# GpSimd's order fixed to the source's, the statistics placed behind a scan, and the next chunk's preparation shifted by half a state

## The chip, the core and the metric

The kernel runs on one core of a Trainium2 chip. The core has five engines that each work through a queue of their own, in order: PE (TensorE, matrix products; its weight loads are shown as PEld), DVE (VectorE), ACT (ScalarE), POOL (GpSimd) and SP (SyncE, which only issues transfers here). An instruction waits at the head of its queue until the semaphores it needs are set, and everything behind it waits with it. The metric is the time on the device in microseconds (us).

## What is computed

A net of four layers on an input of 4 images, 128 channels, 64 x 64 pixels. The change lies in the part of the program that computes the first two layers together. Layer 0 is a state space model (256 inner channels, 16 states) over the 4096 pixels of an image, and layer 1 a hypergraph convolution; cut to what matters here:

```python
# layer 0, per image
xc    = silu(conv(xs) + conv_b)
x_dbl = xc @ x_proj_w.T                      # 8 + 16 + 16 rows: dt, B, C
delta = softplus(dt_r @ dt_proj_w.T + dt_proj_b)
hn = exp(delta * A) * hprev + (delta * xc) * B_t     # for each of 16 states, along the pixels
y  = sum over states of hn * C_t
x  = ((y + xc * D) * silu(zg)) @ out_proj_w.T + x
# layer 1, per image, on the normalized x
incidence = (dist < THRESHOLD)               # 4096 x 4096
edge = incidence^T @ xe / deg_e
vert = incidence @ edge / deg_v
out  = vert + xf
y = batchnorm(out)                           # mean and variance over all images
x = x + y * sigmoid(y)
```

Layers 2 and 3 (attention and experts) follow and are not touched.

## The kernel before

`layers01` (from L79) is one program of Python generators. `layer0()` (L378) yields after each half state: an image is cut into 8 chunks of 512 columns, a chunk has 16 states, and a state has two halves `h` of 128 channels each. `layer1(b, ...)` (L469) yields the weight of the work that it has just emitted. The driver at L697 to L723 first emits image 0 of layer 0 alone; then, for images 1 to 3 of layer 0, it emits one half state, raises `self.tick` by one, runs the deferred pieces that are due, and emits as much of layer 1 of the image before as belongs to that half state; at last layer 1 of image 3 alone. In this text chunks of layer 0 are counted through from 0 to 31, so image 1 starts with chunk 8.

For a state `n` of a chunk:

- `rows` (L280) loads B and C of the state, repeated over the partitions, into `bt` on SP's queue, three states ahead; there are five buffers.
- `drive` (L289) makes `db` = `dx` x B on GpSimd, one state ahead; `db` has two buffers, so that of state j+2 needs both scans of state j done.
- `state` (L293) makes two exponentials into the PSUM tile `hs` on ScalarE (L303; two buffers), a scan for each half on VectorE (L309), and after the second one a copy of the last column (`carry`, L318) and the product `ho` = `hs` x C (L319). For images 1 to 3 GpSimd then adds `ho` to the running sum of its eight states (L324, L326); states 0 and 8 only start a sum. For image 0 six of the sixteen products are GpSimd's (L314, L315).
- `steps` (L390) hangs the rest of layer 0 on half states `u` = 0 to 31 of a chunk. The list `slots` gives the half states in which the eleven steps that prepare the next chunk are emitted: load, project, conv, small (the small projection's matrix products, L242), rows_out (its copy L246 on ScalarE, and the store that `rows` of the next chunk reads), delta, two activations, exp, ln, and inputs (L271 and L273 on GpSimd: `dl` and `dx` for the next chunk).

Layer 1 of an image has a part in which token blocks are prepared, compared (L541 on PE, L544 on VectorE) or turned from earlier results (L553, L557), with the edge sums of the panel before (L564, L571 to L582) between them; and a vertex part (L654 on) that works through 8 column chunks. GpSimd's share in it is: the remainder of the tokens in half precision (L506), the scaling of the edges `ed` (L580), their remainder (L582), and the addition of the input to the vertex result `rb` (L681). ScalarE's L581 waits for L580. VectorE's product L680, GpSimd's L681 and VectorE's statistics L684 follow each other; L680 and L681 are emitted one tick after a column chunk's matrix products, L684 six ticks after them.

What sets the order in each queue: a planner of the framework orders the instructions of each engine by when it believes them ready, with the source's order as the priority. ScalarE is an exception: each of its instructions in this part is passed through `act` (L187), which makes it depend on the one before, for the order alone and with no semaphore. PE, VectorE, GpSimd and SP are left to the planner. So the source's place of an instruction is not its place in the queue.

Of the kernel before, what the change touches and what calls it, by code (L numbers as in the profile page):

```python
# [12 lines left out]
ALU = mybir.AluOpType  # L13
# [4 lines left out]
P = 128  # L18
# [13 lines left out]
def bc(ap, n):  # L32

    return ap.unsqueeze(1).to_broadcast([ap.shape[0], n, ap.shape[1]])
# [7 lines left out]
class Net:  # L42
# [36 lines left out]
    def layers01(self):  # L79
# [11 lines left out]
        with ExitStack() as ctx:  # L91
# [90 lines left out]
            late = ctx.enter_context(tc.tile_pool(name="late", bufs=1))  # L182


            order = []

            def act(i):  # L187


                if order:  # L190
                    tc.add_manual_dep(
                        i.ins, order[-1].name,
                        mybir.DependencyInfo(mybir.DependencyClass.NoSync, mybir.DependencyReason.DATA),
                        reason="order",
                    )
                order[:] = [i.ins]


            waiting = []
# [11 lines left out]
            def before(b, c):  # L211

                s = dict(b=b, c=c)
                t0 = c * T

                def load():
                    xt = s["xt"] = w2.tile([P, T + 3], F32, tag="xt", name="xt")
                    if c == 0:
                        nc.vector.memset(xt[:, 0:3], 0.0)
                        nc.sync.dma_start(xt[:, 3:], a["x"][b, :, 0:T])  # L220
                    else:
                        nc.sync.dma_start(xt, a["x"][b, :, t0 - 3 : t0 + T])

                def project():
                    xt = s["xt"]
                    s["ps"] = [ps.tile([P, T], F32, tag="ps", name="ps_c") for h in range(2)]
                    for h in range(2):
                        for j in range(4):
                            nc.tensor.matmul(  # L229
                                s["ps"][h], wc[:, h, j, :], xt[:, j : j + T], start=j == 0, stop=j == 3  # L230
                            )

                def conv():
                    xc = s["xc"] = w2.tile([P, 2, T], F32, tag="xc", name="xc")
                    for h in range(2):
                        act(nc.scalar.activation(xc[:, h, :], s["ps"][h], AF.Silu, bias=vec[:, h, 4:5]))

                def small():
                    xc = s["xc"]
                    px = s["px"] = ps.tile([P, T], F32, tag="ps", name="ps_xd")  # L240
                    for h in range(2):
                        nc.tensor.matmul(px[:40, :], xpT[:, h, :], xc[:, h, :], start=h == 0, stop=h == 1)  # L242

                def rows_out():
                    xd = s["xd"] = w2.tile([40, T], F32, tag="xd", name="xd", bufs=1)
                    act(nc.scalar.copy(xd, s["px"][:40, :]))  # L246
                    bcd = s["bcd"] = dp.tile([2 * DS, T], F32, tag="bcd", name="bcd")
                    nc.scalar.dma_start(bcd, xd[DR:40, :])

                def delta():  # L250
                    s["ps"] = [ps.tile([P, T], F32, tag="ps", name="ps_d") for h in range(2)]
                    for h in range(2):
                        nc.tensor.matmul(s["ps"][h], dtT[:, h, :], s["xd"][0:DR, :], start=True, stop=True)


                def parts(h):
                    if h == 0:
                        s["dl"] = w2.tile([P, 2, T], F32, tag="dl", name="dl")
                        s["sp"] = late.tile([P, 2, T], F32, tag="sp", name="sp")
                    act(nc.scalar.activation(s["sp"][:, h, :], s["ps"][h], AF.Abs, bias=vec[:, h, 5:6]))  # L260
                    act(nc.scalar.activation(s["dl"][:, h, :], s["ps"][h], AF.Relu, bias=vec[:, h, 5:6]))

                def exp():
                    act(nc.scalar.activation(s["sp"], s["sp"], AF.Exp, scale=-1.0))

                def ln():
                    act(nc.scalar.activation(s["sp"], s["sp"], AF.Ln, bias=1.0))

                def inputs():
                    dl = s["dl"]  # L270
                    nc.gpsimd.tensor_tensor(dl, dl, s["sp"], ALU.add)  # L271
                    dx = s["dx"] = w2.tile([P, 2, T], F32, tag="dx", name="dx")
                    nc.gpsimd.tensor_tensor(dx, dl, s["xc"], ALU.mult)  # L273

                return s, [
                    load, project, conv, small, rows_out, delta, lambda: parts(0), lambda: parts(1), exp, ln,
                    inputs,
                ]

# [8 lines left out]

            def drive(s, n):  # L289
                db = s["db", n] = w2.tile([P, 2, T], F32, tag="db", name="db")  # L290
                nc.gpsimd.tensor_tensor(db, s["dx"], bc(s["bt", n][:, 0, :], 2), ALU.mult)  # L291

            def state(s, n, h):  # L293

                b, c, db = s["b"], s["c"], s["db", n]
                if h == 0:
                    hs = s["hs"] = aps.tile([P, 2, T], F32, tag="hs", name="hs")  # L300
                    s["ho", n] = w2.tile([P, 2, T], F32, tag="ho", name="ho", bufs=6)
                    for k in range(2):
                        act(nc.scalar.activation(hs[:, k, :], s["dl"][:, k, :], AF.Exp, scale=A[:, k, n : n + 1]))  # L303
                hs, ho = s["hs"], s["ho", n]
                ct = bc(s["bt", n][:, 1, :], 2)
                split = b == 0 and n in TO_POOL
                init = 0.0 if c == 0 else carry[:, n, h : h + 1]
                to = ho if split else hs
                nc.vector.tensor_tensor_scan(to[:, h, :], hs[:, h, :], db[:, h, :], init, ALU.mult, ALU.add)  # L309
                if h == 0:  # L310
                    return
                if split:
                    if c < NT - 1:
                        nc.gpsimd.tensor_copy(carry[:, n, :], ho[:, :, T - 1])  # L314
                    nc.gpsimd.tensor_tensor(ho, ho, ct, ALU.mult)  # L315
                    return
                if c < NT - 1:
                    nc.vector.tensor_copy(carry[:, n, :], hs[:, :, T - 1])  # L318
                nc.vector.tensor_tensor(ho, hs, ct, ALU.mult)  # L319
                if b == 0 or n % G == 0:  # L320
                    return
                if n % G == 1:
                    s["sum", n // G] = w2.tile([P, 2, T], F32, tag="ho", name="ho_s", bufs=6)
                    nc.gpsimd.tensor_tensor(s["sum", n // G], ho, s["ho", n - 1], ALU.add)  # L324
                else:
                    nc.gpsimd.tensor_tensor(s["sum", n // G], s["sum", n // G], ho, ALU.add)  # L326

            def skip(s):

# [48 lines left out]
            def layer0():  # L378
# [6 lines left out]
                count = len(todo) * DS  # L385
                at = lambda i: (todo[i // DS][0], i % DS)

                slots = dict(zip((9, 14, 16, 18, 19, 20, 22, 23, 24, 25, 26), range(11)))

                def steps(k, u):  # L390

# [77 lines left out]
            def layer1(b, rstd, nmr):  # L469
# [18 lines left out]
                def tokens(c, sq):  # L488
# [14 lines left out]
                    hi = xs[:, 4 * c : 4 * c + 4, 0:P]  # L503
                    lo = xs[:, 4 * c : 4 * c + 4, P + 1 : 2 * P + 1]
                    later(2, lambda: act(nc.scalar.copy(hi, xe)))
                    later(3, lambda: nc.gpsimd.tensor_tensor(lo, xe, hi, ALU.subtract))  # L506

                def row(c, sq=None):

# [49 lines left out]
                def edges(inc, ed, c, i):  # L559
# [9 lines left out]
                    def parts():  # L569
                        both = pe[:, : 2 * P + 2].rearrange("p (k c) -> p c k", k=2)  # L570
                        nc.vector.reduce_sum(ed[:, i, :], both, axis=AX.X)  # L571
                        if i == 3:

                            rd = rdeg[:, 4 * c : 4 * c + 4]
                            nc.vector.tensor_scalar(rd, ed[:, :, P], 1.0, None, ALU.max)
                            nc.vector.reciprocal(rd, rd)  # L576
                            e = ed[:, :, :P]
                            hi = es[:, 4 * c : 4 * c + 4, 0, :]
                            lo = es[:, 4 * c : 4 * c + 4, 1, :]
                            nc.gpsimd.tensor_tensor(e, e, bc_last(rd, P), ALU.mult)  # L580
                            later(3, lambda: act(nc.scalar.copy(hi, e)))  # L581
                            later(4, lambda: nc.gpsimd.tensor_tensor(lo, e, hi, ALU.subtract))  # L582

                    later(2, parts)

# [68 lines left out]
                for c in range(NCH):  # L654
# [23 lines left out]

                    def mean(c=c, rb=rb, pv=pv):
                        nc.vector.scalar_tensor_tensor(rb, pv, top, rb, ALU.mult, ALU.mult)  # L680
                        nc.gpsimd.tensor_tensor(rb, rb, xn[c], ALU.add)  # L681

                    def finish(c=c, rb=rb):
                        nc.vector.bn_stats(stats[:, b, c, :], rb)  # L684
                        nc.sync.dma_start(self.hg[b][:, c * CH : (c + 1) * CH], rb)

                    due()
# [874 lines left out]
```

## Time and profile before

| | us |
|---|---|
| median of three runs | 4104.38 (4102.41 to 4105.93) |
| profiled execution, its own time | 4105.69 |
| its span | 4103.9 |
| layer 0 of image 0 alone | 45 to 562 |
| layer 0 of images 1 to 3 beside layer 1 of images 0 to 2 | 562 to 2824 |
| layer 1 of image 3 alone | 2824 to 3312 |
| layers 2 and 3 | 3312 to 4104 |
| busy in all: PE, DVE, ACT, POOL | 3456.7, 3001.7, 2034.9, 2460.4 |

The times of the stages are from the span's start. In the middle stage each of PE, VectorE and GpSimd is busy for about 82% of the time, but not at the same places: the stage repeats itself once for each image, 754 us long, and every image has a stretch of its own for comparing, for the edges and for the vertices. A row of waits reads: the engine and the instruction that waited, the engine and the instruction that ended the wait, the sum in us, how often, the longest. In the timeline the idle time before an instruction stands in brackets, with what ended it.

### The profile page before, as it was taken

What the parts mean: (1) busy time and instruction counts of PE and PEld (TensorE: products, weight loads), DVE (VectorE), ACT (ScalarE), POOL (GpSimd) and SP (SyncE); (2) the same over time, 40 slices, a digit from 0 to 9 for tenths busy, and PEclk for the clock granted to TensorE, in tenths of its full rate; (3) what the DMA queues carried; (4) which work ended last, traced back from release to release, by engine and by line L of the source; (5) the groups of instructions that cost most, each with busy time, mean ns of one, the idle gap of its engine ahead of it and who ended that gap; (6) DMA issues with size and microseconds to landing.
All of it is one profiled execution on the core that took longest, in us unless ns stands there. A gap on an engine that the chain in (4) does not pass through costs nothing. (4 is left out here: it accounts for less than half of the span.)

```text
span 4103.9 us, 48550 instructions
## 1 busy us (share of the span) xinstructions
PE 3456.7 (84%) x17255; PEld 1931.4 (47%) x17255; DVE 3001.7 (73%) x4628; ACT 2034.9 (50%) x3364; POOL 2460.4 (60%) x1242
## 2 busy tenths in 40 slices
PE   6878767888889788888977888887999979998989
PEld 2323323344543334455433444543567448765864
DVE  5888889999666899975679998664642067665764
ACT  4556554445644555555444455642223158842951
POOL 5998989888678898986879888674100020001300
PEclk8898888899999899999988999999999989999999
DMA  3545544455436454543644455447121420046138
GB/s 101 149 148 155 151 122 126 130 143 152 118 123 199 116 139 130 147 138 87 213 135 130 131 146 145 115 134 246 52 73 55 127 100 11 12 140 218 27 109 298
DMA packets 263845, 532.71 MB, mean 130 GB/s; under 512 B 22794, under 2 KB 25266, under 8 KB 262578
## 3 DMA queue, kind: packets, MB, share of 16 engines
q1 hardware_dynamic: 255666, 519.09, 42.3%
q10 hardware_dynamic: 7936, 10.52, 0.7%
q8 instruction: 136, 2.23, 0.2%
q14 instruction: 107, 0.88, 0.1%
HBM read 451.80 MB, written 77.73 MB: 129 GB/s over the span
## 5 line engine op out<-in xcount | busy, mean ns | idle before, releaser
L291 POOL TENSOR_TENSOR db<-dx,bt 128x1024 f32<-128x1024 f32 x512 | 1202.9, 2352 | 349.5 <-DVE hs L309 204.4
L309 DVE TENSOR_TENSOR_SCAN hs<-hs,carry,db 128x512 f32<-128x512 f32 x812 | 1033.9, 1282 | 257.1 <-ACT hs L303 176.0
L303 ACT ACTIVATE hs<-dl,A 128x512 f32<-128x512 f32 x1024 | 706.0, 692 | 773.1 <-DVE ho L319 721.2
L541 PE MATMUL ps_g<-xn 128*128 128x512 f32 x1152 | 603.5, 654 | 121.3 <-DVE inc L544 95.3
L326 POOL TENSOR_TENSOR ho_s<-ho_s,ho 128x1024 f32<-128x1024 f32 x288 | 677.5, 2352 | 11.7 <-DVE ho L319 6.5
L319 DVE TENSOR_TENSOR ho<-hs,bt 128x1024 f32<-128x1024 f32 x464 | 563.3, 1214 | 1.6
L564 PE MATMUL ps_ed<-xs,inc 128*128 128x258 f16 x4096 | 508.8, 284 | 41.8 <-DVE inc L544 20.2
L564 PEld LDWEIGHTS <-inc 128*128 128x128 fp8e4 x4096 | 414.7, 102 | 160.5 <-issue 88.8
L544 DVE SCALAR_TENSOR_TENSOR inc<-ps_g,hcl,hb 128x512 fp8e4<-128x512 f32 x576 | 418.6, 735 | 26.3 <-PE ps_g L541 12.6
L541 PEld LDWEIGHTS ps_g<-xn 128*128 128x128 f32 x1152 | 214.4, 203 | 439.3 <-DVE inc L544 213.1
L557 ACT CAST inc<-ps_t 128x512 fp8e4<-128x512 f32 x448 | 231.7, 601 | 299.3 <-PE ps_t L553 277.5
L347 PE MATMUL ps_y<-ho,cst 128*128 128x512 f32 x512 | 274.6, 680 | 108.9 <-POOL ho L315 91.5
L672 PE MATMUL ps_v<-inc_v,es 128*128 128x512 fp8e4 x1536 | 344.9, 383 | 18.0 <-DVE rb L680 18.0
L672 PEld LDWEIGHTS <-es 128*128 128x128 f16 x2048 | 203.2, 100 | 287.8 <-issue 65.2
L229 PE MATMUL ps_c<-xt,wc 128*128 128x512 f32 x512 | 234.2, 611 | 4.1 <-DVE inc L544 2.1
L347 PEld LDWEIGHTS ps_y<-ho,cst 128*128 128x128 f32 x512 | 105.5, 215 | 269.0 <-POOL ho L315 121.9
L1231 POOL CAST b1h<-b 128x512 bf16<-128x512 f32 x2 | 1.3, 648 | 302.1 <-DMA b<-in_L_ffn_weight 302.1
L580 POOL TENSOR_TENSOR ed<-ed,rdeg 128x512 f32<-128x512 f32 x32 | 33.2, 1038 | 247.6 <-DVE rdeg L576 247.6
L309 DVE TENSOR_TENSOR_SCAN hs<-hs,db 128x512 f32<-128x512 f32 x116 | 141.3, 1223 | 43.4 <-POOL db L291 36.9
L571 DVE TENSOR_REDUCE ed<-ps_ed 128x129 f32<-128x258 f32 x128 | 52.9, 413 | 159.5 <-PE ps_ed L564 159.5
L229 PEld LDWEIGHTS ps_c<-xt,wc 128*128 128x128 f32 x512 | 99.3, 197 | 127.7 <-issue 114.9
L1467 POOL MEMSET ob<- 128x256 f32 x4 | 1.2, 311 | 262.1 <-PE ps_t L1410 262.1
(317 smaller groups left out, 5463.7 us busy)
## 6 DMA issues: line engine op xcount, KB each, us to landing
bt<-bcd SPq DMA_DIRECT2D x512, 512.0 KB, 4.9
w<-in_L_ffn_weight SPq DMA_DIRECT2D x64, 1024.0 KB, 11.1
inc<-inc SPq DMA_DIRECT2D x192, 256.0 KB, 2.4
inc_v<-inc SPq DMA_DIRECT2D x96, 512.0 KB, 6.4
strip<-inc SPq DMA_DIRECT2D x84, 256.0 KB, 3.0
x<-x ACTq DMA_DIRECT2D x32, 256.0 KB, 5.7
xn<-x SPq DMA_DIRECT2D x32, 256.0 KB, 5.5
hg<-rb SPq DMA_DIRECT2D x32, 256.0 KB, 2.7
```

The source lines that it names most:

```text
L229: nc.tensor.matmul(s["ps"][h], wc[:, h, j, :], xt[:, j : j + T], start=j == 0, stop=j == 3)
L291: nc.gpsimd.tensor_tensor(db, s["dx"], bc(s["bt", n][:, 0, :], 2), ALU.mult)
L303: act(nc.scalar.activation(hs[:, k, :], s["dl"][:, k, :], AF.Exp, scale=A[:, k, n : n + 1]))
L309: nc.vector.tensor_tensor_scan(to[:, h, :], hs[:, h, :], db[:, h, :], init, ALU.mult, ALU.add)
L319: nc.vector.tensor_tensor(ho, hs, ct, ALU.mult)
L326: nc.gpsimd.tensor_tensor(s["sum", n // G], s["sum", n // G], ho, ALU.add)
L347: nc.tensor.matmul(s["y"][h], self.ident, t[:, h, :], start=False, stop=n == DS - 1 and k == len(terms) - 1,)
L541: nc.tensor.matmul(pq, xn[v // 4][:, v % 4 * P : (v % 4 + 1) * P], xn[c], start=True, stop=True)
L544: nc.vector.scalar_tensor_tensor(inc[:, v, :], pq, hc[:, v : v + 1], hb, ALU.subtract, ALU.is_gt, saturate=False)
L557: later(1, lambda: act(nc.scalar.copy(inc[:, v, :], pt, saturate=False)))
L564: nc.tensor.matmul(pe[:, : 2 * P + 2], inc[:, v, i * P : (i + 1) * P], xs[:, v, :], start=v == 0, stop=v == NB - 1,)
L672: nc.tensor.matmul(pv, es[:, e, k, :], inc[:, e, :], start=e == 0 and k == 0, stop=e == NB - 1 and k == 1,)
```

## The change

Three edits, all in `layers01`. The first gives GpSimd what ScalarE has: each of its instructions from the moment that `self.tick` is above zero (that is, from the start of layer 1 of image 0) depends on the one emitted before it, for the order alone. It holds for the eight places at which GpSimd works in this part. The second makes the vertex statistics depend, again for the order alone, on the scan that was emitted last before them. The third moves the steps from `rows_out` on in `slots` by one half state; the matrix products of the small projection keep their place.

```diff
-            order = []
+            def follow(i, j):
+                tc.add_manual_dep(
+                    i.ins, j.name,
+                    mybir.DependencyInfo(mybir.DependencyClass.NoSync, mybir.DependencyReason.DATA),
+                    reason="order",
+                )
+            order = {}
+            def in_order(engine, i):
+                if engine in order:
+                    follow(i, order[engine])
+                order[engine] = i.ins
             def act(i):
...
+                in_order("act", i)
+            def pool(i):
+                if self.tick:
+                    in_order("pool", i)
...
-                    nc.gpsimd.tensor_tensor(dl, dl, s["sp"], ALU.add)
+                    pool(nc.gpsimd.tensor_tensor(dl, dl, s["sp"], ALU.add))
...
-                nc.gpsimd.tensor_tensor(db, s["dx"], bc(s["bt", n][:, 0, :], 2), ALU.mult)
+                pool(nc.gpsimd.tensor_tensor(db, s["dx"], bc(s["bt", n][:, 0, :], 2), ALU.mult))
...
-                nc.vector.tensor_tensor_scan(to[:, h, :], hs[:, h, :], db[:, h, :], init, ALU.mult, ALU.add)
+                i = nc.vector.tensor_tensor_scan(to[:, h, :], hs[:, h, :], db[:, h, :], init, ALU.mult, ALU.add)
+                order["scan"] = i.ins
...
-                    nc.gpsimd.tensor_tensor(s["sum", n // G], s["sum", n // G], ho, ALU.add)
+                    pool(nc.gpsimd.tensor_tensor(s["sum", n // G], s["sum", n // G], ho, ALU.add))
...
-                slots = dict(zip((9, 14, 16, 18, 19, 20, 22, 23, 24, 25, 26), range(11)))
+                slots = dict(zip((9, 14, 16, 18, 20, 21, 23, 24, 25, 26, 27), range(11)))
...
-                            nc.gpsimd.tensor_tensor(e, e, bc_last(rd, P), ALU.mult)
+                            pool(nc.gpsimd.tensor_tensor(e, e, bc_last(rd, P), ALU.mult))
...
-                        nc.gpsimd.tensor_tensor(rb, rb, xn[c], ALU.add)
+                        pool(nc.gpsimd.tensor_tensor(rb, rb, xn[c], ALU.add))
                     def finish(c=c, rb=rb):
-                        nc.vector.bn_stats(stats[:, b, c, :], rb)
+                        follow(nc.vector.bn_stats(stats[:, b, c, :], rb), order["scan"])
                         nc.sync.dma_start(self.hg[b][:, c * CH : (c + 1) * CH], rb)
```

The places left out (L273, L314, L315, L324, L506 and L582) get the same `pool(...)` around them.

More of the change, by code (lines that the diff above doesn't have):

```diff
@@ L182, in layers01 @@
             late = ctx.enter_context(tc.tile_pool(name="late", bufs=1))
-            order = []
-            def act(i):
[L190 to L196, printed above, removed]
+            def follow(i, j):
[9 more added lines that the diff above has]
+                order[engine] = i.ins
+            def act(i):
+                in_order("act", i)
+            def pool(i):
+                if self.tick:
+                    in_order("pool", i)
             waiting = []
@@ L270, in inputs @@
                     dl = s["dl"]
-                    nc.gpsimd.tensor_tensor(dl, dl, s["sp"], ALU.add)
+                    pool(nc.gpsimd.tensor_tensor(dl, dl, s["sp"], ALU.add))
                     dx = s["dx"] = w2.tile([P, 2, T], F32, tag="dx", name="dx")
-                    nc.gpsimd.tensor_tensor(dx, dl, s["xc"], ALU.mult)
+                    pool(nc.gpsimd.tensor_tensor(dx, dl, s["xc"], ALU.mult))
                 return s, [
@@ L313, in state @@
                     if c < NT - 1:
-                        nc.gpsimd.tensor_copy(carry[:, n, :], ho[:, :, T - 1])
-                    nc.gpsimd.tensor_tensor(ho, ho, ct, ALU.mult)
+                        pool(nc.gpsimd.tensor_copy(carry[:, n, :], ho[:, :, T - 1]))
+                    pool(nc.gpsimd.tensor_tensor(ho, ho, ct, ALU.mult))
                     return
@@ L323, in state @@
                     s["sum", n // G] = w2.tile([P, 2, T], F32, tag="ho", name="ho_s", bufs=6)
-                    nc.gpsimd.tensor_tensor(s["sum", n // G], ho, s["ho", n - 1], ALU.add)
+                    pool(nc.gpsimd.tensor_tensor(s["sum", n // G], ho, s["ho", n - 1], ALU.add))
                 else:
-                    nc.gpsimd.tensor_tensor(s["sum", n // G], s["sum", n // G], ho, ALU.add)
+                    pool(nc.gpsimd.tensor_tensor(s["sum", n // G], s["sum", n // G], ho, ALU.add))
             def skip(s):
@@ L505, in tokens @@
                     later(2, lambda: act(nc.scalar.copy(hi, xe)))
-                    later(3, lambda: nc.gpsimd.tensor_tensor(lo, xe, hi, ALU.subtract))
+                    later(3, lambda: pool(nc.gpsimd.tensor_tensor(lo, xe, hi, ALU.subtract)))
                 def row(c, sq=None):
@@ L579, in parts @@
                             lo = es[:, 4 * c : 4 * c + 4, 1, :]
-                            nc.gpsimd.tensor_tensor(e, e, bc_last(rd, P), ALU.mult)
+                            pool(nc.gpsimd.tensor_tensor(e, e, bc_last(rd, P), ALU.mult))
                             later(3, lambda: act(nc.scalar.copy(hi, e)))
-                            later(4, lambda: nc.gpsimd.tensor_tensor(lo, e, hi, ALU.subtract))
+                            later(4, lambda: pool(nc.gpsimd.tensor_tensor(lo, e, hi, ALU.subtract)))
                     later(2, parts)
```

## The prediction

> **What bounds the kernel now.** I read the page's groups first, then the waits of each engine between 562 and 2824 us, where layer 0 of images 1 to 3 runs beside layer 1 of images 0 to 2 and where nearly all of the change lies, then the busy time by stretch, then the timeline.
>
> ```profile
> L291 POOL TENSOR_TENSOR db<-dx,bt 128x1024 f32<-128x1024 f32 x512 | 1202.9, 2352 | 349.5 <-DVE hs L309 204.4
> L309 DVE TENSOR_TENSOR_SCAN hs<-hs,carry,db 128x512 f32<-128x512 f32 x812 | 1033.9, 1282 | 257.1 <-ACT hs L303 176.0
> ```
>
> A state costs GpSimd one `db` of 2.352 us and mostly one sum (L326) of the same length: 4.7 us. It costs VectorE two scans of 1.28, a product of 1.21 and a carry of 0.15: 3.9 us, plus layer 1's work. GpSimd's largest idle is for a scan (a `db` buffer comes free), so it runs ahead.
>
> ```profile
> 1403.00:1571.00 168.00, 133.28 (x430) 60.90 (x429) 160.63 (x205) 83.49 (x114) 156.60 (x72) 0.90 0.49 132
> 1571.00:1747.00 176.00, 146.55 (x667) 78.43 (x667) 164.30 (x209) 94.62 (x139) 154.17 (x70) 0.92 0.50 143
> ...
> 1845.00:1938.00 93.00, 73.93 (x500) 49.43 (x499) 55.02 (x70) 43.59 (x76) 57.41 (x28) 0.92 0.34 92
> 1938.00:2108.00 170.00, 153.78 (x595) 66.31 (x593) 117.18 (x122) 74.97 (x117) 135.97 (x62) 0.94 0.63 186
> ```
>
> The columns are the stretch, its length, then busy time of PE, PEld, DVE, ACT and POOL. In the first two (compare phase, chunks 17 to 20; a chunk is 512 columns of layer 0, eight to an image, counted through) VectorE is 93 to 96% busy and GpSimd 88 to 93%: two coupled engines without slack. In the third (last edges) nobody is above 80%: latency. In the fourth (vertex phase) PE leads with 154 of 170 us.
>
> ```profile
> DVE hs L309 <- ACT hs L303: 180.9, 66, 9.4
> DVE stats L684 <- POOL rb L681: 102.0, 21, 8.9
> ...
> DVE hs L309 <- POOL db L291: 24.5, 26, 1.9
> ```
>
> ```profile
> ACT es L581 <- POOL ed L580: 129.3, 23, 10.0
> ACT xd L246 <- PE ps_xd L242: 64.7, 23, 6.4
> ```
>
> Three of these waits are touched: the statistics, the scaled edges, the copy of the small projection. The small one, scan for `db`, is the one to watch.
>
> **Part 1: statistics (L684) behind a scan.** The timeline shows the stall:
>
> ```profile
> 1979.29 0.74 DVE L680 SCALAR_TENSOR_TENSOR rb<-ps_v,top,rb 128x512 f32<-128x512 f32 x1
> ...
> 1980.09 2.08 PE L332 MATMUL ps_y<-xc,dD 128*128 128x512 f32 x2 [4.59 <-DVE rb L680]
> ...
> 1982.85 1.26 POOL L681 TENSOR_TENSOR rb<-rb,xn 128x512 f32<-128x512 f32 x1
> ...
> 1984.15 0.69 DVE L684 BATCH_NORM_STATS2 stats<-rb 128x6 f32<-128x512 f32 x1 [4.12 <-POOL rb L681]
> ```
>
> VectorE sits at L684 for 4.12 us while GpSimd does a `db` and a sum before the addition; three ready scans are queued behind. The source emits L684 five half states after L680, so with the new dependency it stands behind scans that take longer than the addition needs: I take the whole 102.0 us off VectorE. That is not 102 us off the time, because in this phase PE leads. PE's idle time that is due to VectorE here is 4.6 us (above) and 8.6 us (a wait of L672 for L680, whose queue was held by earlier stalls) in each of two images, and 4.4 + 8.2 in the third: 39 us. Ends 0 and 48 (all 16 us of idle, three times); I take 30, since L680 still waits for its place.
>
> A rule of the Trainium skill speaks against this move. SBUF — State Buffer, section "Summary: rules for kernel authors", says that a VectorE instruction in a 2-port mode, or with two SBUF inputs while GpSimd reads SBUF, is blocked until the other engine has finished. In before, L684 mostly ran with GpSimd just done; moved, it runs beside `db`. If it were blocked, 24 of them would lose up to 2.35 us: 56 us.
>
> ```profile
> L375 DVE BATCH_NORM_STATS2 stats<-x x32: 661/682/696, 129.1 to 2833.8; 128x6 f32<-128x512 f32 x32
> ...
> L575 DVE TENSOR_SCALAR rdeg<-ed x32: 155/802/2153, 784.3 to 3184.0; 128x4 f32<-128x4 f32 x32
> ```
>
> These rows (minimum, median, maximum in ns) are from two questions, by line. L575, a small operation from SBUF to SBUF, shows such blocking: 0.16 us alone, up to 2.15 beside a `db` that ends with it. L375 is the same statistics instruction as L684, ran beside a busy GpSimd 23 times of the 31 before 2824 us, and never took over 0.70 us. By the rule +56, by the row 0; I take the row.
>
> **Part 2: GpSimd in source order.** No instruction is added: `db`, sums, inputs and layer 1's four kinds (L506, L580, L582, L681, 24 each in this stretch) keep their durations. Matching GpSimd's trace with the source's order, line by line: in before the `db` stand 0.7 places earlier than in the source, the sums 1.3 later, `ed` (L580) 1.4 later, the addition (L681) 0.9 later, `dl` and `dx` 2.3 and 1.2 earlier. So the pin helps `ed` and the addition, and hurts every `db`. The addition is counted in part 1.
>
> *Gain at `ed`.* ScalarE waits 129.3 us for it, with the exponentials of the scans behind. In the last edges of an image (chunks 14, 22, 30) three such waits are 8.5 to 9.9 us, where VectorE waits 23.5 us for exponentials. One place earlier is 2.35 us, three times in three images: 21 us. PE's edge sums share that chain, so I take half, 10; ends 0 and 21. Where VectorE is full, the wait is covered by exponentials already made.
>
> *Loss at `db`.* In the source, `db` of state j+1 comes first, then the sum of j, then `db` of j+2, and so on. Until now `db` went ahead as soon as a scan freed its buffer. From now on, `db` of j+1 stands behind the sum of j-1, and that waits for the product of j-1. Chunk 18 shows what it costs, VectorE first, GpSimd below:
>
> ```profile
> 1494.47 1.22 DVE L319 TENSOR_TENSOR ho<-hs,bt 128x1024 f32<-128x1024 f32 x1
> ...
> 1497.43 2.46 DVE L309 TENSOR_TENSOR_SCAN hs<-hs,carry,db 128x512 f32<-128x512 f32 x2
> ```
>
> ```profile
> 1491.88 4.65 POOL L291 TENSOR_TENSOR db<-dx,bt 128x1024 f32<-128x1024 f32 x2
> 1496.49 2.34 POOL L324 TENSOR_TENSOR ho_s<-ho 128x1024 f32<-128x1024 f32 x1
> ```
>
> State 1's product ends at 1495.69. The second scan of the x2 (state 3) starts at 1498.65; its `db` was the second of GpSimd's x2, from 1494.18. In source order the sum goes first, 1495.69 to 1498.1, then `db` to 1500.4: the scan is 1.75 us late. The need is 2.35 + 2.35 + 0.1 = 4.8 us from a product to the scan two states on. I read that interval for every state: in chunks 8 to 12, 17 to 20 and 25 to 28, 74 of 195 are shorter, by 31.5 + 22.5 + 22.5 = 76.5 us. These 13 chunks are the ones where VectorE has almost no idle time (2.5 to 8.7 us each, 60.8 in all), so lateness adds to the time. At a chunk's end `dl` and `dx` (4.7 us) make GpSimd continuous; states 14 and 15 have a median slack of 0.0 and 0.3 us between `db` and scan, and one more sum now stands ahead: 2.35 x 13 = 31, of which I count half, 15, since those states are partly in the 76.5. Half of the idle time takes lateness up: -30 (ends 0 and -61; an earlier layer-1 operation of VectorE can fill the hole too). In the other 11 chunks intervals are short by 60 us, but VectorE idles 18 to 52 us in each: a quarter, 15. Loss: 76.5 + 15 - 30 + 15 = 76.
>
> **Part 3: from the small projection's copy on, one half state later.** The matrix products (L242) stay; the copy (L246), its store on ScalarE's queue, `delta`, the four activations, exponential, logarithm and the inputs shift. The copy then stands behind one more exponential, so PE gets some 2.9 us more; ScalarE's 64.7 us of waits nearly vanish (2.8 each). But ScalarE runs up to two states ahead, and VectorE's waits before state 10's scans, which stand behind that copy, total only 9.3 us: gain 6, ends 0 and 9. The stored rows are wanted by SP's loads three states after, 18 us; a `bt` lands in 4.9 us: no cost, unless SP's queue, in order, is held longer by the first load of a chunk, with strips behind it. The inputs now follow the sum of state 13; that sum is in the 15 above.
>
> **Sum.** 76 - 30 - 10 - 6 = +30 us. The profiled execution took 4105.7 us (span 4103.9 and 1.8 around it): 4135.7. The median of the runs shown is 1.3 below it: **4134 us**, slower by 0.7%. No change is within 0.2%, about 8 us, which is what runs of this kernel can tell apart.
>
> **Rivals.**
> *A, forecast (44%):* the lost head start of `db` outweighs the removed stalls, +8 to +85 us.
> *B, the stalls win (34%):* the compiled order of VectorE adapts, all 61 us of idle time and the layer-1 work absorb lateness: loss 30. Gains at their upper values, 39 + 21 + 9 = 69: 4104 - 39 = 4065. For it: 102 + 129 + 65 us of waits are really removed. Against: they lie on engines that don't lead where they occur.
> *C, GpSimd becomes the bound in the compare phase (12%):* nothing is absorbed, 76.5 + 31 + 15 = 122, gains 20: 4206. For it: 32 operations of 2.35 and some 5 us for layer 1 make 80 us of chunk 17's 82.7. It decides from the point where a sum and a `db` no longer fit between product and scan. Against: the 7% of idle time.
> *D, nothing to measure (10%):* both balance, or the order of other engines changes little: 4104.
>
> **Range.** The low end reaches past B's 4065 to 4050 (gains 69 with a loss of 15), the high end to C's 4206: about 8% below and 8% above are left out. A's own range is 4112 to 4189. Slower: A and C, 0.56; same 0.10; faster 0.34.
>
> **What would show it.** Right: VectorE's wait for L681 near zero; GpSimd's largest idle moves from "db for a scan" to "sum for a product" (L326 for L319); VectorE's wait for `db` grows from 24.5 to 90 us or more; chunks 17 to 20 grow by 3 to 6 us each, the vertex phase falls from 170 to about 160. Wrong: `db` waits stay near 25 us, or the compare phase doesn't grow; then B holds.

## The result and the profile after

The changed kernel takes 4235.25 us (4231.39 to 4237.65), the kernel before 4105.16 in the same session: a ratio of 1.0316, 95% interval 1.0298 to 1.0334. It is slower, as forecast, but by 130 us where 30 were forecast, and outside the range (4050 to 4206).

First the page's groups of the changed kernel (scan L322, `db` L304, sum L340):

```profile
L322 DVE TENSOR_TENSOR_SCAN hs<-hs,carry,db 128x512 f32<-128x512 f32 x812 | 1041.7, 1286 | 467.4 <-POOL db L304 302.6
L304 POOL TENSOR_TENSOR db<-dx,bt 128x1024 f32<-128x1024 f32 x512 | 1201.0, 2350 | 14.8 <-issue 8.0
...
L340 POOL TENSOR_TENSOR ho_s<-ho_s,ho 128x1024 f32<-128x1024 f32 x288 | 676.6, 2349 | 272.9 <-DVE ho L333 272.4
```

None of these instructions became slower by more than 0.4%. The idle time ahead of the scans of this row rose from 257 to 467 us, and what ends most of it is no longer ScalarE's exponential but GpSimd's `db`. GpSimd in turn no longer waits ahead of `db` (349.5 us before, 14.8 now) but ahead of the sum, for VectorE's product. The waits of VectorE and GpSimd in the shared stage (562 to 2958 us) say the same:

```profile
DVE hs L322 <- POOL db L304: 298.9, 153, 5.8
DVE hs L322 <- ACT hs L316: 163.2, 55, 7.6
...
DVE stats L699 <- POOL rb L695: 2.7, 2, 1.4
```

```profile
POOL ho_s L340 <- DVE ho L333: 272.4, 144, 6.8
POOL ho_s L338 <- DVE ho L333: 97.3, 35, 5.0
```

VectorE's wait for `db` went from 24.5 to 298.9 us; its wait ahead of the statistics went from 102.0 to 2.7. The place in chunk 18 on which the prediction worked out its 1.75 us looks like this now, in the timeline of VectorE and of GpSimd:

```profile
1543.80 1.28 DVE L322 TENSOR_TENSOR_SCAN hs<-hs,carry,db 128x512 f32<-128x512 f32 x1
...
1545.70 1.22 DVE L333 TENSOR_TENSOR ho<-hs,bt 128x1024 f32<-128x1024 f32 x1
...
1548.67 1.28 DVE L322 TENSOR_TENSOR_SCAN hs<-hs,carry,db 128x512 f32<-128x512 f32 x1
1551.69 1.29 DVE L322 TENSOR_TENSOR_SCAN hs<-hs,carry,db 128x512 f32<-128x512 f32 x1 [1.74 <-POOL db L304]
```

```profile
1547.00 2.36 POOL L338 TENSOR_TENSOR ho_s<-ho 128x1024 f32<-128x1024 f32 x1 [3.10 <-DVE ho L333]
1549.31 2.35 POOL L304 TENSOR_TENSOR db<-dx,bt 128x1024 f32<-128x1024 f32 x1
```

GpSimd stands idle for 3.10 us. For the last 1.9 of them the `db` of state 3 could have been computed, since the second scan of state 1 (at 1543.80) had ended at 1545.08 and freed its buffer; but it stands behind the sum. Then GpSimd does both, and VectorE waits 1.74 us.

Where the 130 us lie, from the starts of the scans in the two traces (lengths in us; a chunk lasts from its first scan to that of the next):

| | before | after |
|---|---|---|
| from the span's start to chunk 8 (image 0 alone) | 548.0 | 544.2 |
| the 13 chunks in which VectorE was full (8 to 12, 17 to 20, 25 to 28) | 1121.2 | 1231.0 |
| the 11 other chunks (13 to 16, 21 to 24, 29 to 31) | 1152.9 | 1180.5 |
| from the last scan on | 1281.8 | 1275.6 |

### The profile page after: what moved, and what is told of

It is laid out like the page before. It is cut to its first block, busy times and chain, and to the rows that moved or that the text cites. A ratio compares the mean times of both kernels' runs of the same rounds, so it can differ in the third digit from the quotient of the medians.

```text
span 4231.3 us, 48315 instructions
## 1 busy us (share of the span) xinstructions
PE 3489.0 (82%) x17255; PEld 1956.1 (46%) x17255; DVE 2988.0 (71%) x4628; ACT 2036.1 (48%) x3364; POOL 2460.2 (58%) x1242
## 5 line engine op out<-in xcount | busy, mean ns | idle before, releaser
L322 DVE TENSOR_TENSOR_SCAN hs<-hs,carry,db 128x512 f32<-128x512 f32 x812 | 1041.7, 1286 | 467.4 <-POOL db L304 302.6
L304 POOL TENSOR_TENSOR db<-dx,bt 128x1024 f32<-128x1024 f32 x512 | 1201.0, 2350 | 14.8 <-issue 8.0
L340 POOL TENSOR_TENSOR ho_s<-ho_s,ho 128x1024 f32<-128x1024 f32 x288 | 676.6, 2349 | 272.9 <-DVE ho L333 272.4
L555 PE MATMUL ps_g<-xn 128*128 128x512 f32 x1152 | 613.8, 664 | 154.0 <-DVE inc L558 112.7
L578 PE MATMUL ps_ed<-xs,inc 128*128 128x258 f16 x4096 | 533.8, 293 | 49.0 <-DVE inc L558 36.7
L578 PEld LDWEIGHTS <-inc 128*128 128x128 fp8e4 x4096 | 428.5, 105 | 180.0 <-issue 96.6
L338 POOL TENSOR_TENSOR ho_s<-ho 128x1024 f32<-128x1024 f32 x48 | 113.0, 2354 | 162.4 <-DVE ho L333 97.3
L322 DVE TENSOR_TENSOR_SCAN hs<-hs,db 128x512 f32<-128x512 f32 x116 | 141.6, 1225 | 77.4 <-POOL db L304 71.5
L567 PE MATMUL ps_t<-ident,strip 128*128 128x128 fp8e4 x1344 | 119.3, 235 | 81.3 <-DVE ed L585 51.1
L585 DVE TENSOR_REDUCE ed<-ps_ed 128x129 f32<-128x258 f32 x128 | 53.4, 417 | 165.6 <-PE ps_ed L578 165.6
```

The source lines that it names most:

```text
L304: pool(nc.gpsimd.tensor_tensor(db, s["dx"], bc(s["bt", n][:, 0, :], 2), ALU.mult))
L322: i = nc.vector.tensor_tensor_scan(to[:, h, :], hs[:, h, :], db[:, h, :], init, ALU.mult, ALU.add)
L340: pool(nc.gpsimd.tensor_tensor(s["sum", n // G], s["sum", n // G], ho, ALU.add))
L555: nc.tensor.matmul(pq, xn[v // 4][:, v % 4 * P : (v % 4 + 1) * P], xn[c], start=True, stop=True)
L578: nc.tensor.matmul(pe[:, : 2 * P + 2], inc[:, v, i * P : (i + 1) * P], xs[:, v, :], start=v == 0, stop=v == NB - 1,)
```

## The experiments

My theory: `db` behind the sum is the whole loss. Rival 1: the shift by half a state makes the next chunk's inputs late. Rival 2: the later statistics cost. Rival 3: any fixed order costs, because GpSimd then waits at its head for layer 1's results (3a), or because the planner, given the order, arranges VectorE and PE differently. All times are medians; the kernel before took 4102.6, 4103.1 and 4101.8 us in the three sessions.

### Each edit alone, and two without the order

**GpSimd's order alone.**

```diff
-                slots = dict(zip((9, 14, 16, 18, 20, 21, 23, 24, 25, 26, 27), range(11)))
+                slots = dict(zip((9, 14, 16, 18, 19, 20, 22, 23, 24, 25, 26), range(11)))
...
-                        follow(nc.vector.bn_stats(stats[:, b, c, :], rb), order["scan"])
+                        nc.vector.bn_stats(stats[:, b, c, :], rb)
```

> GpSimd's order alone, without the other two edits. Theory (each `db` now stands behind a sum that waits for VectorE's product): nearly the whole loss is here, 4225 to 4265 us, VectorE waits over 250 us for `db`; the statistics' wait of 102 us is still there or smaller, as the addition comes earlier. Rival 1 (the shift by half a state makes the inputs late): 4100 to 4150. Rival 2 (the later statistics hold the buffers of rb): 4100 to 4150 as well.

4266.1 us, 1.0397 (1.0382 to 1.0413) of before: the loss is here, 163 us, more than the whole change shows. VectorE's waits in the shared stage:

```profile
DVE hs L322 <- POOL db L304: 246.2, 129, 5.4
DVE hs L322 <- ACT hs L316: 155.2, 55, 7.1
DVE stats L699 <- POOL rb L695: 52.1, 21, 6.0
```

With the order the wait for the addition falls by half, from 102 to 52 us. It is a poor trade.

**The statistics alone.** The order is switched off and the half states are the old ones:

```diff
-                if self.tick:
+                if False:
                     in_order("pool", i)
```

> The statistics behind a scan alone. Theory: VectorE's 102 us of waits for the addition vanish, and PE's idle time in the vertex phase with them: 4065 to 4100 us. Rival 2 (the later statistics hold the buffers of rb, or meet GpSimd's reads): 4120 or more. If the gain is taken by another wait in the same phase: 4100 to 4110.

4047.5 us, 0.9863 (0.9848 to 0.9877): a gain of 55 us, more than expected, and rival 2 falls. The busy time of the vertex phase of the second image, before and with this edit (columns as in the prediction; the last three are the granted clock of PE, the share of the DMA engines and GB/s):

```profile
1938.30:2108.00 169.70, 153.48 (x595) 66.27 (x593) 117.18 (x122) 74.97 (x117) 135.97 (x62) 0.94 0.63 186
```

```profile
1916.60:2069.10 152.50, 148.34 (x595) 65.17 (x593) 114.33 (x122) 75.39 (x117) 135.71 (x62) 0.98 0.70 207
```

The phase is 17.2 us shorter. PE's idle pauses of over 0.4 us in it fall from 16.0 to 3.9 us, and its busy time falls by 5.1 us for the same instructions, with the granted clock up from 0.94 to 0.98. From their first matrix product to their last the three vertex phases shrink by 17.2, 17.3 and 18.9 us, 53.4 in all: that is nearly the whole gain.

**The shift alone.** Order and dependency of the statistics off.

> The shift alone. Theory: 4095 to 4105 us, ScalarE's wait before the copy of the small projection falls from 65 us to under 35. Rival 1 (late inputs): 4130 or more, with VectorE's wait for `db` at the ends of chunks up by 20 us or more.

4100.8 us, 0.9995 (0.9987 to 1.0004): no difference that can be measured. The wait that it was to shorten did become shorter, from 64.7 us to

```profile
ACT xd L259 <- PE ps_xd L255: 30.8, 17, 4.2
```

and nothing came of it. Rival 1 falls.

**Statistics and shift, without the order.**

> The changed kernel without GpSimd's order: statistics and shift together. Theory: 4060 to 4100 us, VectorE's wait for `db` near 25 us again. Rivals 1 and 2: 4180 or more.

4054.3 us, 0.9879 (0.9862 to 0.9895). So the order costs 181 us beside the other two edits (4235.3 less 4054.3), and 163 without them.

### Which part of the order

**Each sum behind the next `db`.** The order stays fixed, statistics and shift stay; the sum of a state is kept back until the next state's `db` has been emitted:

```diff
-                if n % G == 1:
...
-                    pool(nc.gpsimd.tensor_tensor(s["sum", n // G], s["sum", n // G], ho, ALU.add))
+                held.append(lambda: pool(nc.gpsimd.tensor_tensor(s["sum", n // G], other, ho, ALU.add)))
...
                     if i + 1 < count:
                         drive(*at(i + 1))
+                    while held:
+                        held.pop(0)()
                     state(*at(i), 0)
```

> The changed kernel, GpSimd's order still fixed, but each sum is emitted behind the next state's `db` instead of ahead of it. Theory (it is the place of `db` behind the sum that costs): the loss goes, 4040 to 4110 us, VectorE's wait for `db` under 80 us. Rival 3 (any fixed order costs, since GpSimd then waits at its head for layer 1's scaling and addition, or since the planner puts VectorE's and PE's work in another order): 4180 or more.

4034.8 us, 0.9829 (0.9815 to 0.9844). Swapping two neighbours in GpSimd's list takes 200 us off the changed kernel and makes it 1.7% faster than before. So a fixed order as such need not cost anything: rival 3 falls as the cause of the loss, including the planner's part in it, since this version is planned anew under a fixed order too. VectorE waits in the shared stage:

```profile
DVE hs L323 <- ACT hs L317: 164.4, 57, 7.1
DVE hs L323 <- POOL db L305: 84.8, 51, 3.3
```

The wait for `db` is somewhat over the 80 us that I had written down, and above the 24.5 of before. The rest of the lateness comes from layer 1's instructions in the order, not from the order of `db` and the sums: when layer 1 is left to the planner (the last version below), it falls to 41.4 us, near the 39.1 of the kernel without any GpSimd order:

```profile
DVE hs L323 <- POOL db L305: 41.4, 34, 2.2
```

That version is not faster for it, since it loses at `ed` what it gains here.

**Only layer 0 in the order.** `pool` is taken off L506's, L580's, L582's and L681's instructions.

> The changed kernel, with only layer 0's GpSimd instructions in the fixed order; layer 1's four kinds are left to the planner. Theory: `db` is still behind the sum, so the loss stays, 4210 to 4270 us. Rival 3a (GpSimd's waits at its head for layer 1's rdeg and rb, 75 + 15 us in the changed kernel, are the loss): 4100 to 4160.

4240.9 us, 1.0333 (1.0316 to 1.0350): the loss stays, rival 3a falls. GpSimd still waits for VectorE's products:

```profile
POOL ho_s L340 <- DVE ho L333: 287.4, 142, 8.2
POOL ho_s L338 <- DVE ho L333: 95.7, 30, 7.0
```

**The sums out of the order.** `pool` is taken off the two sums alone; `db`, inputs and layer 1 stay in it.

> The changed kernel, with the sums taken out of the fixed order; `db`, inputs and layer 1's four kinds stay in it. Theory: the planner puts `db` ahead of the sum again, 4040 to 4100 us. Rival 3a: 4180 or more, since `db` still stands behind the scaling of the edges.

4057.2 us, 0.9886 (0.9871 to 0.9901), beside 4054.3 without any order: the loss is gone as soon as the sums may stand where the planner puts them. VectorE still waits 107.5 us for `db` here (39.1 without any order) at almost the same time, so a sum of waits is not yet time.

**Half the dose.** As with all sums behind `db`, but those of states 9 to 15 go ahead of it again:

```diff
                 held.append(lambda: pool(nc.gpsimd.tensor_tensor(s["sum", n // G], other, ho, ALU.add)))
+                if n >= G:
+                    held.pop()()
```

> Half the dose: sums of states 1 to 7 of a chunk behind the next `db`, those of states 9 to 15 ahead of it as in the changed kernel. Theory (each sum ahead of a `db` costs in its own place): between 4035 and 4235, about 4120 to 4160, with VectorE's waits for `db` in the second half of the chunks only. If only the crowded end of a chunk matters (inputs, states 14 to 1): 4200 or more; if it is not the sums: near 4035 or near 4235.

4154.2 us, 1.0127 (1.0112 to 1.0142), between 4034.8 (none ahead) and 4235.3 (all ahead). In the changed kernel the sum of a state stands ahead of the `db` of the state two on, so the sums of states 1 to 7 bear on the scans of states 3 to 9, and those of states 9 to 15 on states 11 to 15 and on 0 and 1 of the next chunk. VectorE's idle time ahead of the scans, added up over the 24 shared chunks (us):

| scans of states | none ahead | half ahead | all ahead |
|---|---|---|---|
| 3 to 9 | 125.1 | 123.5 | 213.3 |
| 11 to 15, and 0 and 1 of the next chunk | 138.0 | 253.2 | 255.5 |
| of these, state 15 alone | 44.0 | 111.7 | 111.3 |

The lateness comes where a sum stands ahead of a `db`, and nowhere else. The second half costs more (119 us of the 200), and more than half of its rise lies at state 15: ahead of that state's `db` stand the inputs for the next chunk, `dl` and `dx`, in all three versions, but the head start of `db` that covers them is gone where the sum comes first: at state 14 a `db` ends 3.1 us (median) ahead of its scan with no sum ahead, and 0.04 us in the other two.

### What of the rest pays

**Sums behind `db`, without the shift.** The old list of half states:

> Sums behind the next `db`, fixed order, statistics behind a scan, but the old half states for the next chunk's preparation. Theory: the shift is worth nothing by itself (4100.8 beside 4102.6 alone; 4054 with, 4048 without it beside the statistics), so 4025 to 4045, and it should be the fastest version or equal to it. If the shift only pays with a fixed order: 4050 or more.

4038.8 us, 0.9842 (0.9825 to 0.9858), which is the 4034.8 with the shift within what can be told apart. The shift may be left out.

**Sums behind `db`, layer 1 left to the planner.**

> As the version with sums behind `db` (4034.8), but layer 1's four GpSimd kinds are left to the planner. It tells where that version's 20 us over the version without any GpSimd order (4054.3) come from. If from the place of layer 1's scaling `ed` (ScalarE waits for it in the edge phase): 4050 to 4065 and chunk 22 near 117 us. If from the fixed places of `db` and sums: 4030 to 4045 and chunk 22 near 109 us.

4043.3 us, 0.9858 (0.9844 to 0.9873): the time is in the second band, the chunks are as in the first. Chunk 22 takes 117.4 us here and 109.4 with layer 1 in the order, chunks 14 and 30 117.5 and 117.3 against 110.6 and 110.8: 21 us from the place of `ed`, in the edge phase. Some 9 of them are lost again in other chunks, so that the two profiled executions are 12 us apart and the medians 8, at the edge of what can be told. My two readings weren't exclusive. ScalarE's wait for the scaled edges, with layer 1 left to the planner and with layer 1 in the order:

```profile
ACT es L601 <- POOL ed L600: 130.1, 24, 10.3
```

```profile
ACT es L601 <- POOL ed L600: 73.9, 24, 5.6
```

So 56 us of ScalarE's wait are worth 21 us where they lie and about 8 us in the end.

## Why the prediction was right in its direction and wrong in its size

**The mechanism** was named: `db` behind a sum that waits for a product. The interval that it needs and the example of chunk 18 (1.75 us forecast, 1.74 measured) hold. So do the direction and the rows of waits that were to show it: the statistics' wait near zero, GpSimd's largest idle time ahead of the sum, VectorE's wait for `db` far over 90 us.

**The step that failed is the size of the loss at `db`, 76.5 + 15 - 30 + 15 = 76 us.** With the 10 us gained at `ed` the order was to cost 66 us; it cost 181. The other two edits brought 48 us (4102.6 less 4054.3) where 36 were forecast, and 181 - 48 = 133 is about the 130 measured. By chunks, the changed kernel against the one without the order: the 13 full chunks 1231.0 against 1129.9, so 101 us where 76.5 + 15 - 30 = 61 were forecast; the other 11 chunks 1180.5 against 1094.6, so 86 us where "a quarter, 15" was forecast. Between these two kernels VectorE's idle time ahead of the scans rose by (us):

| ahead of the scans of | 13 full chunks | 11 other chunks |
|---|---|---|
| state 15 | 51.7 | 36.5 |
| all other states | 51.6 | 66.8 |

Two terms were too small.

*The chunk's end.* It was put at 15 us (31 at most) in the 13 chunks and at nothing in the other 11; 52 and 37 came. The prediction counted one more sum of 2.35 us there, and half of it. But from the product of state 13 to the scan of state 15, VectorE first and GpSimd below, there now lie a sum, `dl`, `dx` and a `db` (chunk 18):

```profile
1621.48 1.22 DVE L333 TENSOR_TENSOR ho<-hs,bt 128x1024 f32<-128x1024 f32 x1
1627.08 1.29 DVE L322 TENSOR_TENSOR_SCAN hs<-hs,carry,db 128x512 f32<-128x512 f32 x1 [4.39 <-POOL db L304]
```

```profile
1617.65 2.36 POOL L340 TENSOR_TENSOR ho_s<-ho_s,ho 128x1024 f32<-128x1024 f32 x1
1619.97 2.36 POOL L284 TENSOR_TENSOR dl<-dl,sp 128x1024 f32<-128x1024 f32 x1
1622.40 2.34 POOL L286 TENSOR_TENSOR dx<-dl,xc 128x1024 f32<-128x1024 f32 x1
1624.70 2.34 POOL L304 TENSOR_TENSOR db<-dx,bt 128x1024 f32<-128x1024 f32 x1
```

The interval of 4.8 us that was used for every state is too short for this one: it needs 4 x 2.35 + 0.1 = 9.5 us. In before the interval is 4.2 to 9.2 us in the 13 chunks. With 9.5 in place of 4.8 for this state the prediction's own way of reading gives 43.5 us there and 26 in the others (an estimate from the trace of before) instead of 15 and nothing. What is left to the 52 and 37 stays open.

*The quarter for the other 11 chunks.* Of the 86 us that came, 36.5 lie at state 15; the other 49 (66.8 ahead of the scans, less 17 of VectorE's other waits that fell) stand against the 60 us of short intervals, of which three quarters were to vanish in VectorE's idle time. Most of that idle time was a wait for exponentials: 174 us without the order, and 140 of them are still there with it. ScalarE's exponential waits for a PSUM buffer that VectorE's product frees (667.8 us of waits in the shared stage of the changed kernel), so a late `db` makes the scan, the product and the next exponential late in turn, and the pause moves along instead of being used up. That this is the reason is argued from the rows; no run took it apart.

In the 13 full chunks the rest of the sum was about right: 76.5 - 30 = 46.5 us forecast, 51.6 measured. So the 30 us taken off for idle time were not the error there, though no run shows what took them up. The sign that chunks 17 to 20 would grow by 3 to 6 us each failed with the chunk's end: they grew by 5.1, 10.2, 8.9 and 10.6 us.

**Rival C was the nearest in its number, 4206, but not in its mechanism.** It made GpSimd the bound of the compare phase. In chunks 17 to 20 of the changed kernel (columns as in the prediction) GpSimd is busy for 82% and VectorE for 86% of the time, less than the 90 and 94% of before: the two wait for each other in turn.

```profile
1448.90:1827.80 378.90, 289.62 (x1097) 145.48 (x1097) 324.31 (x413) 178.04 (x253) 311.33 (x141) 0.88 0.43 125
```

**The statistics** were undervalued: 30 us (ends 0 and 48), measured 55. The wait vanished as forecast. PE's pauses in the three vertex phases gave some 36 us, near the 39 that I had counted before I took less; the other 17 or so are busy time of PE, which fell as its granted clock rose, and which I had left out. In the changed kernel the vertex phase shows none of this; it is no shorter than before:

```profile
2019.40:2192.20 172.80, 153.87 (x599) 66.56 (x597) 115.50 (x122) 75.02 (x117) 136.37 (x63) 0.94 0.59 183
```

There VectorE's 35.5 us of waits for the addition had become 35.1 us of waits for `db`: a new wait in the place of the one removed. The forecast of "about 160" for this phase fails with it. Statistics and shift together still take 31 us off the kernel with the order alone (4266.1 against 4235.3), about half of them in the 13 full chunks; which of the two does it there, no run shows.

**The rule of the Trainium skill against the statistics' move** was rightly set aside, and as the prediction quotes it, it did not forecast the 56 us: it speaks of a 2-port mode or of two inputs in SBUF, and the statistics instruction reads one tile. Whether it runs in such a mode no run shows, but it was not blocked: 21 of the 32 in the changed kernel ran beside a busy GpSimd, and none took over 0.70 us:

```profile
L699 DVE BATCH_NORM_STATS2 stats<-rb x32: 667/670/695, 1245.8 to 3441.4; 128x6 f32<-128x512 f32 x32
```

**The scaled edges**, 10 us (ends 0 and 21): 21 in the edge chunks, but about 8 in all where `db` has its head start (4043.3 against 4034.8), 6 in the changed kernel (4240.9 against 4235.3). Right within what can be told apart.

**The shift**, 6 us (ends 0 and 9): 1.8 us alone, not to be told from nothing. The lower end.

## What to carry to other kernels

Where two engines hand work to each other, the order of two neighbours in one queue decides: an instruction that only collects a result (a sum) should not stand ahead of one that the other engine will wait for next (an input). Here the swap was worth 200 us of 4235. Before an order is fixed, look for each instruction at what it waits for and at who waits for what stands behind it; here a fixed order with the inputs first was harmless, and even paid. When the need is worked out as an interval, count everything that stands in the queue between its two ends, place by place: at the end of a chunk it was four instructions and not two, and that was the largest error. And idle time of the engine that is made late is a poor reserve, if that idle time is itself a wait in the same ring.

## What was not expected of the hardware

PE's granted clock was higher where PE stopped less: in the vertex phase it went from 0.94 to 0.98 when its pauses fell from 16.0 to 3.9 us of 170 and 152, and its busy time for the same 595 matrix products fell by 3%. So some 5 of the 17 us gained in this phase are shorter busy time, and not the pauses themselves. With the order (172.8 us, 19 us of such pauses) the clock was 0.94 again. What makes the clock follow the stops, these runs don't show.
